# A layered attention kernel with a new order inside each slot: output product and residual in front of the Q projection, and a norm's second parts moved up

## The chip, the cores and the metric

The kernel runs on one core of one Trainium2 chip. The metric is the device time of one execution in microseconds (us). A core has five engines with a queue of instructions each: TensorE (PE in the profile; its weight loads are shown apart as PEld), VectorE (DVE), ScalarE (ACT), GpSimd (POOL) and SyncE (SP), which here issues DMAs. Every engine works its own queue strictly in order, and waits at an instruction until what that needs is there.

## The reference

The input x has 4 sequences (B) of 512 tokens with 128 features. First comes one block of full attention with 16 heads of 64 on a layer norm of x:

```
x = x + softmax(mask(q k^T / 8)) v Wr        with q, k, v = layernorm(x) Wq, Wk, Wv
```

Then x plus the result of six layers. In a layer i, `shift` moves half of the features of each token one token on:

```
q, k, v = split(shift(x) Wqkv[i])                       16 heads of 64
q, k    = rotary(q / |q| * q_scale), rotary(k / |k| * k_scale)
x       = x + local_attention(q, k, v) Wo[i]            windows of 32, each sees itself and the one before
h       = layernorm(shift(x)) * g + b
x       = x + ((h W1a + b1a) * gelu(h W1g + b1g)) W2 + b2
```

All of it is in float32. The change concerns only the six layers.

## The kernel before, in words

Before the layers runs the full attention, up to about 559 us into the span. The layers work in units: a unit is one block of 128 tokens, and there are 6 layers x 4 sequences x 4 blocks = 96 units, numbered n = 0 to 95, in the order layer, sequence, block. T is a unit's block in its sequence (n mod 4), and NT is 4.

The function `slot(n, ...)` is called for n = -1 to 94, and is a software pipeline over units written out by hand: the order of the calls in it is the order of the instructions in each engine's queue (`tc.manual_schedule`), and no planner changes it. In slot n, four units are at work:

- `u` = unit n: its scores (TensorE, L681 and L692; maximum and subtraction on VectorE, L702 and L704; exponents on ScalarE, L710), the transposes of its probabilities P (`transpose_p`, two groups of four), and the product with V (`times_v`, two halves g = 0 and 1 of 64 matmuls, each ended by a reciprocal and a division on VectorE, L733 and L734).
- `prev` = unit n - 1: its output product (`project_out_2`, L749) and the residual (`residual`, L757 on VectorE).
- `nxt` = unit n + 1: the transposes of its Q and K.
- `new` = unit n + 2: its Q, K and V projections (`do_project(new, 0)`, `1`, `2`; L536), the squares of Q and K on ScalarE (`square`, L548), the sums of the squares (L553) and the rotation on VectorE (`rotate`: L558, then L564 into a tile t1), which GpSimd adds up (`add_rotated`, L575), and the division by the norm (`inverse_norms`: L579, L81, L82 on VectorE and a chain of small instructions on GpSimd; `over_norm`, L583 on GpSimd).

Beside this a feed-forward network of a whole sequence (`Ffn`) runs over several slots. After its last unit of attention, in a slot with n mod 4 = 0, `f.shift` (the list `move`) copies the shifted sequence on GpSimd. The three steps of its layer norm (`f.mean`, `f.var`, `f.scale`, the list `norm`) follow in the next three slots, n mod 4 = 1, 2, 3. A step has a first part (a matmul and an instruction or so behind it) and a second part, which is put into the list `later` and issued further on in the same slot: for the mean a square on ScalarE (L104), for the variance a reciprocal square root (two VectorE instructions, L81 and L82, and twelve on GpSimd), for the scale a multiplication by g and addition of b on VectorE (L123), which makes hT. The network's three chunks (L793 and L794, the list `geglu`) come near the ends of the slots n mod 4 = 3, 0, 1, the first of them in the slot of the scale, and its output (L813) in n mod 4 = 2. Slots 0, 1 and 2 have the three steps of another norm, that of the first block's last sequence, which uses no `later` list; slot 93 has the mean of a last network. So the slots with a norm step are n mod 4 = 1, 2, 3 (and 0), and those without are n mod 4 = 0 (and 3).

The PSUM buffers matter here. `two_t(k)` gives one of three two-bank buffers, which change their roles from slot to slot; there is one tile of each. In a slot the scores use `two_t(0)`, Q `two_t(1)`, K `two_t(2)`; V and the first half of times_v use `two_t(0)` again, the second half of times_v and the chunk `two_t(1)`:

```
p = u.p[j] if c0 else two_t(((1, 2, 1), (0, 2, 1), (1, 2, 0))[min(u.n, 2)][j], "ps_proj")
...
o = two_t(g, "ps_att")
```

`one_t()` gives one of two single banks (`ps_one`), for transposes, norm steps and output products. A buffer is used again when all that read it are done.

Of the kernel before, what the change touches and what calls it, by code (L numbers as in the profile page):

```python
# [32 lines left out]
def body(ctx: ExitStack, tc: tile.TileContext, a, out: bass.AP):  # L33
# [37 lines left out]
    def new_xT():  # L71
        return res.tile([P, S], F32, tag="xT", name="xT", bufs=B + 2)
# [416 lines left out]
    def load_part(i, j):  # L489

        w = wts.tile([P, INNER], F32, tag=f"wqkv{j}", name=f"wqkv{j}_{i}")
        nc.sync.dma_start(out=w, in_=a["wqkv"][i, :, j * INNER : (j + 1) * INNER])
        return w
# [19 lines left out]
    def two_t(k, name):  # L513
        k = (part[0] + k) % 3
        return (ps2a if k == 2 else ps).tile([P, 2, 512], F32, tag=f"two{k}", name=name, bufs=1)
# [4 lines left out]
    def heads(ap):  # L520
        return ap.rearrange("p (h d) -> p h d", d=HD)
# [10 lines left out]
    def project(u, j, c0=0, c1=2):  # L532
        p = u.p[j] if c0 else two_t(((1, 2, 1), (0, 2, 1), (1, 2, 0))[min(u.n, 2)][j], "ps_proj")
        u.p[j] = p
        for c in range(c0, c1):
            mm(  # L536
                p[:, c, :],
                lhsT=u.xs[:, u.T * P : (u.T + 1) * P],
                rhs=wpart[j][:, c * 512 : (c + 1) * 512],
                start=True,  # L540
                stop=True,
            )
        if c1 == 2:
            u.p[j] = flat(p)

    def square(u, j):
        u.sq[j] = s2a.tile([P, INNER], F32, tag="t1", name="sq", bufs=4)
        nc.scalar.activation(u.sq[j], u.p[j], AF.Square)  # L548
# [3 lines left out]
            u.ss = small.tile([P, 2 * HEADS], F32, tag="ss", name="ss")  # L552
        nc.vector.tensor_reduce(u.ss[:, j * HEADS : (j + 1) * HEADS], heads(u.sq[j]), AX.X, ALU.add)  # L553

    def rotate(u, j, between=()):
        t0 = u.r[j] = s2a.tile([P, INNER], F32, tag="rot", name="rot", bufs=6)
        lt, pf, half = u.lt, u.p[j], HD // 2
        nc.vector.tensor_tensor(  # L558
            heads(t0), heads(pf), lt[:, u.T, 2 * j].unsqueeze(1).to_broadcast([P, HEADS, HD]), ALU.mult
        )  # L560
        for f in between:
            f()
        t1 = u.t1 = s2a.tile([P, INNER], F32, tag="t1", name="t1", bufs=4)
        nc.vector.tensor_tensor(  # L564
            t1.rearrange("p (h t d) -> p h t d", t=2, d=half),
            pf.rearrange("p (h t d) -> p h t d", t=2, d=half)[:, :, ::-1, :],
            lt[:, u.T, 2 * j + 1]
            .rearrange("p (t d) -> p t d", t=2)
            .unsqueeze(1)
            .to_broadcast([P, HEADS, 2, half]),  # L570
            ALU.mult,
        )

    def add_rotated(u, j):
        nc.gpsimd.tensor_tensor(u.r[j], u.r[j], u.t1, ALU.add)  # L575
# [74 lines left out]
    def transposed(src, g, dst, col0):  # L650

        tp = one_t()
        for c in range(4):
            nc.tensor.transpose(  # L654
                tp[:, c * P : (c + 1) * P], src[:, (4 * g + c) * P : (4 * g + c + 1) * P], ident
            )
        nc.scalar.copy(dst[:, 4 * g : 4 * g + 4, col0 : col0 + P], tp.rearrange("p (c t) -> p c t", c=4))  # L657
# [54 lines left out]
    def transpose_p(u, g):  # L712
        if g == 0:
            u.pT = s2.tile([P, NC, P], F32, tag="pT", name="pT", bufs=2)
        transposed(u.prf, g, u.pT, 0)

    def times_v(u, g):
        if g == 0:
            u.on = s2.tile([P, NC, 2, HD], F32, tag="on", name="on", bufs=1)
        o = two_t(g, "ps_att")  # L720
        for c in range(4):
            for j in range(NW):
                for h in range(2):
                    mm(  # L724
                        o[j * W : (j + 1) * W, h, c * (HD + 1) : (c + 1) * (HD + 1)],
                        lhsT=u.pT[h * HD : (h + 1) * HD, 4 * g + c, j * W : (j + 1) * W],
                        rhs=u.vw[h * HD : (h + 1) * HD, j, 4 * g + c, :],
                        start=True,
                        stop=True,
                    )  # L730
        ov = o[:, :, 0 : 4 * (HD + 1)].rearrange("p a (c d) -> p a c d", d=HD + 1)
        rden = small.tile([P, 2, 4, 1], F32, tag="rden", name="rden")
        nc.vector.reciprocal(rden, ov[:, :, :, HD : HD + 1])  # L733
        nc.vector.tensor_tensor(  # L734
            u.on[:, 4 * g : 4 * g + 4].rearrange("p c a d -> p a c d"),
            ov[:, :, :, 0:HD],
            rden.to_broadcast([P, 2, 4, HD]),
            ALU.mult,
        )
# [11 lines left out]
    def residual(u):  # L751
        if u.T == 0:
            u.xn = new_xT()
        else:
            u.xn = units[u.n - 1].xn
        cols = slice(u.T * P, (u.T + 1) * P)
        nc.vector.tensor_tensor(u.xn[:, cols], u.y[:, 0:P], xT[u.b][:, cols], ALU.add)  # L757
        if u.T + 1 == NT:
            xT[u.b] = u.xn
# [86 lines left out]
    def unit(n):  # L846
        return units[n] if 0 <= n < len(units) else None
# [4 lines left out]
    def begin(u):  # L852

        if u is None or u.T:
            return
        if u.n == 0:
            xs, lt = start
        else:
            xs = shifted(u.b)
            lt = layer_tables(u.i) if u.b == 0 else units[u.n - 1].lt  # L860
        for v in units[u.n : u.n + NT]:
            v.xs, v.lt, v.p = xs, lt, [None] * 3

    def do_project(u, j, c0=0, c1=2):
        project(u, j, c0, c1)
        if c1 == 2 and u.b + 1 == B and u.T + 1 == NT and u.i + 1 < L:
            wpart[j] = load_part(u.i + 1, j)
# [30 lines left out]
    def slot(n, norm, move, geglu):  # L898

        u, prev, nxt, new = unit(n), unit(n - 1), unit(n + 1), unit(n + 2)
        part[0] = -n % 3
        begin(unit(n + 4))
        if u:
            scores(u)
            exponents(u)
        while behind:
            behind.pop(0)()  # L910
        if new:
            do_project(new, 0)
            square(new, 0)
        if n == -1:
            y = one_t()
            project_out1(B - 1, y)
        for f in norm:
            f()
        if prev:
            project_out_2(prev)  # L920
            if prev.b + 1 == B and prev.T + 1 == NT and prev.i + 1 < L:
                wo_w[0] = load_wo(prev.i + 1)


        first = u is not None and u.T == 0
        if prev and not first:
            residual(prev)
        if new and first:
            do_project(new, 1, 0, 1)
            rotate(new, 0)  # L930
            add_rotated(new, 0)
        if prev and first:
            residual(prev)
        for f in move:
            f()
        if u:
            transpose_p(u, 0)
        if new:
            do_project(new, 1, 1 if first else 0, 2 if first else 1)
        if u:  # L940
            transpose_p(u, 1)
        if new and not first:
            rotate(new, 0)
            add_rotated(new, 0)
            do_project(new, 1, 1)
        if new:
            square(new, 1)
        if n == -1:
            residual1(B - 1, y)
        if u:  # L950
            times_v(u, 0)
            times_v(u, 1)
        if new:
            sum_squares(new, 0)
            rotate(new, 1, later)
            later.clear()
            add_rotated(new, 1)
            sum_squares(new, 1)
        if nxt:
            transpose_q(nxt)  # L960
        if new:
            do_project(new, 2, 0, 2 if geglu else 1)
        if new and geglu:
            v_windows(new, follower(new))
        if nxt:
            transpose_k(nxt)
        if new and not geglu:
            do_project(new, 2, 1)
            v_windows(new, follower(new))
        if n == -1:  # L970
            third_step()
        if nxt:
            carry_k(nxt, follower(nxt))
        if new:
            norms = [lambda: inverse_norms(new), lambda: over_norm(new, 0), lambda: over_norm(new, 1)]
            if geglu:
                for f in norms:
                    f()
            else:
                behind.extend(norms)  # L980
        for f in geglu:
            f()
        if u:
            transpose_o(u)

    with tc.manual_schedule():
        begin(units[0])
        later, behind = [], []
# [3 lines left out]
        norm, move, geglu = {k: [f] for k, f in enumerate(late)}, {}, {}  # L992
# [8 lines left out]
        for n in range(NT, end - NT, NT):  # L1001
            f = Ffn(units[n - 1], eng=nc.gpsimd, later=later)
# [27 lines left out]
        u, prev = units[end - 1], units[end - 2]  # L1030
# [144 lines left out]
```

## Time and profile before

| | us |
|---|---|
| median of 3 runs | 2208.52 (2208.43 to 2215.15) |
| the profiled execution | 2208.39 |
| its span, from the first instruction to the last | 2206.6 |
| TensorE busy in the span | 2143.0 (97%) |
| VectorE, ScalarE, GpSimd busy | 1697.0, 1360.4, 1507.8 |

The profile is that of one execution; what the span leaves out of its time is 1.8 us. A slot is counted here from its first scores matmul to that of the next slot. Four slots one after the other take 66.9 us:

| slot (n mod 4) | start | us | PE busy | DVE | ACT | POOL |
|---|---|---|---|---|---|---|
| 32 (0) | 1097.14 | 15.96 | 15.88 | 13.59 | 10.83 | 14.20 |
| 33 (1) | 1113.10 | 16.62 | 16.62 | 14.38 | 12.03 | 11.72 |
| 34 (2) | 1129.72 | 17.61 | 17.61 | 14.63 | 10.54 | 12.55 |
| 35 (3) | 1147.33 | 16.71 | 16.42 | 13.17 | 9.82 | 12.87 |

How to read the rows that follow: in a timeline a row has the start, the duration, the engine, the line of the kernel, the operation, the tiles written and read (out<-in), and the number of instructions that were put together in it; square brackets hold the engine's idle time before it and what ended that. In the groups of lines, behind the bar, stand the busy time, the mean time of one in ns, and the idle time before them with its releasers. A row of waits has the total in us, the number, and the longest. The ends of matmuls are modelled, so that a row's start is the better measure: from the start of one row of TensorE to that of the next is what the first one costs. A float32 matmul counts as two instructions, a transpose as one.

### The profile page before, as it was taken

The page shows a single profiled execution, that of the slowest core. Times are in us where ns is not written, and L with a number is a line of the kernel's source. Part 1 is how long each engine was busy: PE and PEld are TensorE (multiplying, and loading weights), DVE is VectorE, ACT ScalarE, POOL GpSimd, SP SyncE. Part 2 cuts the span into 40 slices and gives each one's busy share as a digit, 9 for nine tenths or more (in the row PEclk, how much of TensorE's full clock was granted, in tenths as well). Part 3 has the DMA queues.
Part 4 walks back from the last instruction along what each step waited for, and adds up shares of the span by engine and source line. Part 5 has one row for each costly group of instructions (what it writes and reads, how often), then busy time and mean ns, then how long its engine had stood idle before and what let it go on. Part 6 is the DMA issues. An engine that isn't in the chain of part 4 may idle for free.

```text
span 2206.6 us, 82386 instructions
## 1 busy us (share of the span) xinstructions
PE 2143.0 (97%) x35150; PEld 1433.3 (65%) x35150; DVE 1697.0 (77%) x2501; ACT 1360.4 (62%) x2589; POOL 1507.8 (68%) x2281
## 2 busy tenths in 40 slices
PE   7999999999999999999999999999999999999997
PEld 5665555564666666666676666666666666666665
DVE  4776767676778887888788878887888788888884
ACT  4665656665556666666666666666666666666663
POOL 2554545455778777777777777777777777777772
PEclk9999999999999999999999999999999999999999
DMA  3000000000332233232332323223332223322220
GB/s 120 1 1 1 1 1 1 1 1 3 75 74 65 64 93 74 62 72 65 95 73 62 77 66 101 62 66 74 74 91 66 65 71 87 81 67 68 62 70 26
DMA packets 91063, 125.76 MB, mean 57 GB/s; under 512 B 25422, under 2 KB 39500, under 8 KB 90700
## 3 DMA queue, kind: packets, MB, share of 16 engines
q1 hardware_dynamic: 89996, 118.79, 21.9%
q8 instruction: 280, 4.59, 0.9%
q10 hardware_dynamic: 704, 1.70, 0.2%
q14 instruction: 83, 0.68, 0.1%
HBM read 20.31 MB, written 1.05 MB: 10 GB/s over the span
## 4 chain that ended last, share of the span: by engine, by line
PE 86%; DVE 9%; POOL 2%; issue 2%; ACT 1%; DMA 0%; SPq 0%; POOLq 0%; ACTq 0%; DVEq 0%
PE ps_proj L536 20%; PE ps_one L654 13%; PE ps_one L749 7%; PE ps_att L692 6%; PE ps_sc L296 6%; PE ps_att L724 5%; PE ps_o L381 5%; PE ps_pt L361 5%; PE ps_proj L793 3%; PE ps_proj L813 3%; PE ps_proj L794 3%; DVE rot L558 2%; DVE ss L553 2%; DVE on L734 1%; PE ps_att L681 1%
## 5 line engine op out<-in xcount | busy, mean ns | idle before, releaser
L536 PE MATMUL ps_proj<-wqkv,xs 128*128 128x512 f32 x1152 | 569.5, 602 | 1.9 <-issue 1.8
L575 POOL TENSOR_TENSOR rot<-rot,t 128x1024 f32<-128x1024 f32 x192 | 453.8, 2364 | 166.3 <-DVE t L564 146.1
L350 POOL TENSOR_TENSOR pr<-pr,den 128x1024 f32<-128x1024 f32 x128 | 240.9, 1893 | 246.4 <-DVE den L347 236.6
L583 POOL TENSOR_TENSOR rot<-rot,ss 128x1024 f32<-128x1024 f32 x192 | 361.8, 1905 | 7.4
L558 DVE TENSOR_TENSOR rot<-ps_proj,lt 128x1024 f32<-128x1024 f32 x192 | 233.7, 1217 | 54.5 <-ACT sq L548 54.2
L536 PEld LDWEIGHTS ps_proj<-wqkv,xs 128*128 128x128 f32 x1152 | 188.3, 190 | 104.3 <-issue 94.8
L710 ACT ACTIVATE pr<-pr 128x1024 f32<-128x1024 f32 x96 | 101.5, 1057 | 228.0 <-DVE pr L704 228.0
L564 DVE TENSOR_TENSOR t<-ps_proj,lt 128x1024 f32<-128x1024 f32 x192 | 233.3, 1215 | 0.0
L553 DVE TENSOR_REDUCE ss<-sq 128x16 f32<-128x1024 f32 x192 | 232.1, 1209 | 0.0
L336 ACT ACTIVATE pr<-ps_sc,nm 128x128 f32<-128x128 f32 (+3 forms) x448 | 220.3, 509 | 11.8 <-DVE nm L323 8.6
L654 PEld LDWEIGHTS ps_one<-ident,rot 128*128 128x128 f32 x1536 | 171.8, 141 | 74.1 <-issue 50.6
L654 PE MATMUL ps_one<-ident,rot 128*128 128x128 f32 x1536 | 205.6, 276 | 11.4 <-POOL rot L583 4.7
L548 ACT ACTIVATE sq<-ps_proj 128x1024 f32<-128x1024 f32 x192 | 195.0, 1016 | 34.1 <-PE ps_proj L536 30.7
L323 DVE TENSOR_REDUCE nm<-ps_sc 128x2 f32<-128x1024 f32 x128 | 156.0, 1219 | 62.8 <-PE ps_sc L311 62.8
L749 PEld LDWEIGHTS ps_one<-aT,wo 128*128 128x128 f32 x1536 | 183.9, 193 | 23.7 <-issue 23.0
L749 PE MATMUL ps_one<-aT,wo 128*128 128x128 f32 x1536 | 190.3, 277 | 0.4 <-DVE rs L111 0.3
L84 POOL TENSOR_TENSOR yt<-y 128x32 f32<-128x32 f32 (+2 forms) x384 | 88.2, 230 | 146.3 <-DVE y L82 100.1
L657 ACT COPY pT<-ps_one 128x512 f32<-128x512 f32 x192 | 112.4, 585 | 97.5 <-PE ps_one L654 97.1
L657 ACT COPY qT<-ps_one 128x512 f32<-128x512 f32 x192 | 103.3, 589 | 108.7 <-PE ps_one L654 108.7
L636 ACT COPY vt<-ps_proj 128x512 f32<-128x512 f32 x192 | 103.1, 589 | 99.5 <-PE ps_proj L536 93.1
L702 DVE TENSOR_REDUCE mx<-ps_att 128x16 f32<-128x1024 f32 x96 | 117.3, 1222 | 60.3 <-PE ps_att L692 59.0
L361 PEld LDWEIGHTS ps_pt<-ident,pr 128*128 128x128 f32 x1024 | 117.4, 141 | 58.6 <-issue 47.7
(173 smaller groups left out, 4092.4 us busy)
## 6 DMA issues: line engine op xcount, KB each, us to landing
vw<-vt SPq DMA_DIRECT2D x1152, 65.0 KB
vw_first<-vt SPq DMA_DIRECT2D x336, 65.0 KB
wqkv<-in_wqkv_dram SPq DMA_DIRECT2D x18, 512.0 KB
wo<-in_wo_dram SPq DMA_DIRECT2D x6, 512.0 KB
w<-in_w_dram SPq DMA_DIRECT2D x6, 341.0 KB
xr<-in_x_dram SPq DMA_DIRECT2D x3, 256.0 KB
scales<-in_scales_dram SPq DMA_DIRECT2D x6, 128.0 KB
w<-in_w_dram SPq DMA_DIRECT2D x12, 64.0 KB
```

What stands on the lines that cost most here:

```text
L336: nc.scalar.activation(self.pr[:, h, cols], self.sc[:, h, cols], AF.Exp, bias=self.nm[:, part_, h : h + 1], accum_out=self.den[:, part_, h ...
L350: nc.gpsimd.tensor_tensor(self.pr, self.pr, self.den[:, 0].unsqueeze(2).to_broadcast([P, 2, S]), ALU.mult)
L361: nc.tensor.transpose(pt[:, k * P : (k + 1) * P], self.pr[:, h, k * P : (k + 1) * P], ident)
L536: mm(p[:, c, :], lhsT=u.xs[:, u.T * P : (u.T + 1) * P], rhs=wpart[j][:, c * 512 : (c + 1) * 512], start=True, stop=True,)
L553: nc.vector.tensor_reduce(u.ss[:, j * HEADS : (j + 1) * HEADS], heads(u.sq[j]), AX.X, ALU.add)
L558: nc.vector.tensor_tensor(heads(t0), heads(pf), lt[:, u.T, 2 * j].unsqueeze(1).to_broadcast([P, HEADS, HD]), ALU.mult)
L564: nc.vector.tensor_tensor(t1.rearrange("p (h t d) -> p h t d", t=2, d=half), pf.rearrange("p (h t d) -> p h t d", t=2, d=half)[:, :, ::-1, :],
L575: nc.gpsimd.tensor_tensor(u.r[j], u.r[j], u.t1, ALU.add)
L583: nc.gpsimd.tensor_tensor(heads(u.r[j]), heads(u.r[j]), u.ss[:, j * HEADS : (j + 1) * HEADS].unsqueeze(2).to_broadcast([P, HEADS, HD]), AL ...
L654: nc.tensor.transpose(tp[:, c * P : (c + 1) * P], src[:, (4 * g + c) * P : (4 * g + c + 1) * P], ident)
L657: nc.scalar.copy(dst[:, 4 * g : 4 * g + 4, col0 : col0 + P], tp.rearrange("p (c t) -> p c t", c=4))
L749: mm(y[:, 0:P], lhsT=wo_w[0][:, c, :], rhs=u.aT[:, c, :], start=(c == 0), stop=(c == NC - 1))
```

## The change

The order of the calls in `slot` is changed, and where `later` is issued.

- In a slot with a norm step, the Q projection with its square is issued behind the norm step, the output product and the residual; before, it was in front of them.
- In a slot without one, Q stays in front. The residual is issued directly behind the output product; before, in slots n mod 4 = 0, it came behind the rotation of Q. The rotation of Q and its `add_rotated` come behind both groups of P's transposes, and `move` in front of them; before, in these slots, rotation and addition came between the two halves of K's projection and `move` after them. P's two groups of transposes stand together between the two halves of K; before, the first group was in front of K's second half and the second behind it.
- The second parts of a norm step (`later`) are issued directly behind the divisions of times_v and in front of the sum of Q's squares; before, between the two instructions of the rotation of K.

The diff:

```diff
-    def rotate(u, j, between=()):
+    def rotate(u, j):
...
-        for f in between:
-            f()
...
-        if new:
+        if n == -1:
             do_project(new, 0)
             square(new, 0)
-        if n == -1:
             y = one_t()
             project_out1(B - 1, y)
         for f in norm:
             f()
+        if new and n >= 0 and not norm:
+            do_project(new, 0)
+            square(new, 0)
+
         if prev:
             project_out_2(prev)
             if prev.b + 1 == B and prev.T + 1 == NT and prev.i + 1 < L:
                 wo_w[0] = load_wo(prev.i + 1)
-
-
-        first = u is not None and u.T == 0
-        if prev and not first:
             residual(prev)
-        if new and first:
-            do_project(new, 1, 0, 1)
-            rotate(new, 0)
-            add_rotated(new, 0)
-        if prev and first:
-            residual(prev)
+        if new and n >= 0 and norm:
+            do_project(new, 0)
+            square(new, 0)
         for f in move:
             f()
-        if u:
+        if u and norm:
             transpose_p(u, 0)
         if new:
-            do_project(new, 1, 1 if first else 0, 2 if first else 1)
+            do_project(new, 1, 0, 1)
         if u:
+            if not norm:
+                transpose_p(u, 0)
             transpose_p(u, 1)
-        if new and not first:
+        if new:
             rotate(new, 0)
             add_rotated(new, 0)
             do_project(new, 1, 1)
-        if new:
             square(new, 1)
...
+        while later:
+            later.pop(0)()
         if new:
             sum_squares(new, 0)
-            rotate(new, 1, later)
-            later.clear()
+            rotate(new, 1)
             add_rotated(new, 1)
```

## The prediction

> **What bounds the kernel now.** I read the page first, then the groups of lines, then who waits for the rows of the normalised activations, and last the timeline of one layer's four slots. A slot is the stretch from one unit's scores to the next unit's; I call its kind n mod 4, so slot 33 is kind 1. From the page:
>
> ```profile
> span 2206.6 us, 82386 instructions
> PE 2143.0 (97%) x35150; PEld 1433.3 (65%) x35150; DVE 1697.0 (77%) x2501; ACT 1360.4 (62%) x2589; POOL 1507.8 (68%) x2281
> PE 86%; DVE 9%; POOL 2%; issue 2%; ACT 1%; DMA 0%; SPq 0%; POOLq 0%; ACTq 0%; DVEq 0%
> L558 DVE TENSOR_TENSOR rot<-ps_proj,lt 128x1024 f32<-128x1024 f32 x192 | 233.7, 1217 | 54.5 <-ACT sq L548 54.2
> ```
>
> TensorE sets the end: its own rows fill the chain. A gain can only be a pause of TensorE that goes, a loss only a pause that is made. The last row is the one I build on: the rotation (DVE) does not start when its projection is ready but when ScalarE's square of the same projection is done; 54.2 us of VectorE's idle time end that way. The waits of TensorE, and those on the normalised activations:
>
> ```profile
> PE ps_att L724 <- issue: 11.0, 10, 1.9
> ...
> who waited for it (us, times):
>   PEld ps_proj L793: 10.5, 20
>   PE ps_proj L793: 5.4, 18
> ```
>
> The first row is pauses that no engine causes, all inside the dense 128 matmuls of times_v; the others are the wait for L123 in the kind-3 slots, the one stall that the change can remove. Slot 33, PE, then ACT, then DVE:
>
> ```profile
> 1114.88 1.98 PE L536 MATMUL ps_proj<-wqkv,xs 128*128 128x512 f32 x4
> 1116.70 1.02 PE L100 MATMUL ps_one<-tmp_t,avg 128*128 128x512 f32 x2
> 1117.56 1.95 PE L749 MATMUL ps_one<-aT,wo 128*128 128x128 f32 x16
> 1119.34 0.60 PE L654 MATMUL ps_one<-ident,pr 128*128 128x128 f32 x4
> 1122.03 1.55 PE L724 MATMUL ps_att<-vw,pT 64*32 64x65 f32 x128
> ...
> 1122.20 1.02 ACT L548 ACTIVATE sq<-ps_proj 128x1024 f32<-128x1024 f32 x1 [0.34 <-PE ps_proj L536]
> ...
> 1119.75 1.21 DVE L558 TENSOR_TENSOR rot<-ps_proj,lt 128x1024 f32<-128x1024 f32 x1
> 1120.88 1.21 DVE L564 TENSOR_TENSOR t<-ps_proj,lt 128x1024 f32<-128x1024 f32 x1
> ```
>
> Q occupies TensorE from 1114.88 to 1116.70 (1.82), the mean 0.86, the output product 1.78. The rotation starts at 1119.75, long after its square. Slot 35 (kind 3) and slot 36 (kind 0):
>
> ```profile
> 1160.65 0.54 DVE L123 TENSOR_SCALAR hT<-hT,vecs 128x512 f32<-128x512 f32 x1
> ...
> 1161.25 1.13 PE L793 MATMUL ps_proj<-hT,w 128*128 128x512 f32 x2 [0.29 <-DVE hT L123]
> ...
> 1169.64 1.01 ACT L548 ACTIVATE sq<-ps_proj 128x1024 f32<-128x1024 f32 x1
> ...
> 1170.68 1.23 DVE L558 TENSOR_TENSOR rot<-ps_proj,lt 128x1024 f32<-128x1024 f32 x1 [2.04 <-ACT sq L548]
> ...
> 1171.62 0.42 PEld L654 LDWEIGHTS ps_one<-ident,pr 128*128 128x128 f32 x4 [0.64 <-ACT pT L657]
> ...
> 1171.82 1.21 DVE L564 TENSOR_TENSOR t<-ps_proj,lt 128x1024 f32<-128x1024 f32 x1
> ...
> 1173.15 0.72 PEld L724 LDWEIGHTS ps_att<-vw_first,pT 64*32 64x32 f32 x64 [0.20 <-ACT pT L657]
> ```
>
> In kind 0 the rotation follows the square, and the second half of times_v (64 of 128) starts at 1173.15, 0.12 after L564 ends (1173.03). That is no accident: times_v(u, 1) takes two_t(1), the buffer in which Q stands (project takes two_t(1) for j = 0), and there is one of it. The label names ScalarE's pT copy, done long before; the late one is L564.
>
> **The skill.** "PSUM — Partial Sum Buffer", PSUM bank collisions: two engines must not touch one bank at once, two reads included, and the compiler's scheduler orders them. The trace agrees: in slot 35 the square ends at 1153.80 and the rotation starts at 1153.84. "SBUF — State Buffer", Who interferes with whom: tensor_scalar in a two-port mode and a GpSimd instruction exclude each other for the whole of the one that came first. It agrees: L579 takes 0.17 us at the least and 1.39 in the middle, ending with POOL's L575. "Runtime: NRT & Kernel Launch", Instruction fetch mechanics: the stream comes in 16 KiB blocks, fetched one ahead; the profile has 280 packets on the instruction queue, and the pauses of the first waits row fit blocks used up faster than fetched.
>
> **Part 1: norm slots (kinds 1 to 3), Q behind norm step, output product and residual.** Nothing is added or removed on TensorE: 1.82 + 0.86 + 1.78 end at 1119.34 in either order. But Q now ends at 1119.34 instead of 1116.70, and the buffer is wanted back at the same time as before. The chain from Q's end: 0.17 to the square (1122.03 to 1122.20 in K's case), 1.02 for it, 0.04 to the rotation (slot 35), 2.34 from L558's start to L564's end (1119.75 to 1122.09), 0.15 to TensorE's second half (0.12 to the weights, 0.03 to the matmul). Sum 3.72. TensorE's own work from 1119.34 to that half: 2.69 to times_v at 1122.03 and 0.67 for its first half: 3.36. So it stalls 0.36. Before, L564 ended at 1122.09 and the half began at 1122.70: hidden with 0.46 to spare; the chain moves by 0.82. Queued behind: everything later on TensorE. Kinds 2 and 3 have the same steps from Q's end on, so the same stall. With a Q to project they are slots 0, 1, 2, 5, 6, 7 ... 89, 90, 91 and 93: 70 slots, 70 x 0.36 = +25.2. Bounds 0.30 and 0.40 from the handover times. What else moves is covered: the norm step needs a ps_one bank that aT's copies free in the first 1.7 us of a slot; the residual is done early on VectorE; square(Q) now stands before pT's first copy on ScalarE, which ends some 0.5 later but still over 0.9 before times_v.
> SP: load_part for Q's weights goes behind this Q and its next user also moves back; load_wo stays in a kind-0 slot. The V window DMAs follow V's copies as before. No DMA price.
>
> **Part 2: second parts directly behind the divisions.** Kind 3: L123 no longer stands behind L553 and L558 (1.21 + 1.22), so hT is ready before the FFN chunk. It removes the gap: kT's transposes to L793 take 1.33 in slot 35 (1159.92 to 1161.25) against 0.87 in slot 33, and the first chunk matmul's 0.96 becomes 0.86. 0.56 x 22 such slots = -12.3. Kind 2: the reciprocal root's POOL chain (12 instructions of 0.2) starts some 2.2 us earlier; it lies beside other work, and must, since the norm's transposes now come 1.8 us earlier in the next slot. Kind 1: the square keeps its place on ScalarE. The catch is the port: t now ends in slot 35 near 1156.7 instead of 1156.19, POOL's L575 (2.36) runs to about 1159.1, and L123, due at 1158.7, waits for it. Its own 0.54 becomes 0.5 to 0.9.
>
> **Part 3: kind 0 slots, residual before, P's two groups together.** The second P group no longer waits (0.64 above) and residual's 0.29 leaves the place behind the rotations; but the end of this slot hangs on exponents, square, rotation, second half of times_v, an order that the edit leaves alone. So it gains nothing. Moving the shift's three POOL instructions (1.4) ahead of L575 only delays add_rotated, and POOL's second L575 follows as before. It loses what kind 3 hands on: there VectorE's tail ends 0.3 later (second division waits for the stalled half) plus 0 to 0.4 for the port, while TensorE is 0.36 - 0.56 = -0.20: VectorE is 0.4 to 0.9 further behind, less about 0.1 to 0.2 of slack at L702. Bounds 0 and 0.7; I take 0.3, nearer the lower as the port's hold may end with POOL. 22 x 0.3 = +6.6.
>
> **Part 4: fetch pauses.** A stall inside times_v gives the fetch time: some 13 of the pauses sit there, each up to 0.36 shorter: -4 (bounds -7 and +4, as the stream's alignment to the blocks may also change).
>
> Sum: 25.2 - 12.3 + 6.6 - 4 = +15.5. The profiled execution took 2208.39 (span 2206.6 and 1.8 around it), 0.13 under the median of 2208.52. Forecast 2224.0.
>
> **Rivals.** A (faster): the rotation need not wait for the square. Then the chain is 0.2 + 2.34 + 0.15 = 2.7, below 3.36, no norm slot stalls, 12.3 is gained in kind 3 and about 0.3 x 22 in kind 0: 2208.5 - 19 = 2189. The norm slots stop stalling if the rotation starts within 0.87 of Q's end (3.36 - 2.34 - 0.15), and the sign turns at 1.0, a stall of 0.14; I put it at 1.23. For: in slot 33 the rotation waited for the residual, so not every row shows the square as its release. Against: slots 35 and 36, where nothing else holds it and it starts at the square's end. Chance 0.09.
> B (no change): a shorter handover, a stall of 0.24, and nothing handed to kind 0: 16.8 - 12.3 - 4, about 2209. Chance 0.13.
> C (worse): in kinds 1 to 3 the second P group gets the bank of the first, as in slot 36 today (0.64 row); pT's copy, now behind the square, ends near 1121.1 and that group, due at 1120.64, costs 0.52 in place of 0.36: 70 x 0.16 = +11, 2235. Against: with the residual in front the other bank is free, and slots 33 and 35 show no such wait. Chance 0.08.
>
> **Numbers.** The forecast's case has 0.70, its own range 2214 to 2235 from the bounds of parts 1, 3 and 4. For 8 in 10 I reach a little into B: 2211 to 2236. About 0.3% (6.6 us) is what a measurement of this kernel tells from no change: faster 0.09, same 0.13, slower 0.70 + 0.08 = 0.78.
>
> **What would show it.** Kinds 1 to 3: L558 directly behind its square in most rows, so L558's idle "<-ACT sq" far above 54 us; a gap of about 0.36 between halves of times_v ended by L564; slots of kinds 1 and 2 near 17.0 and 17.9 (16.62 and 17.5 now). Kind 3: no wait on L123, slot 0.2 shorter; L123 longer than 0.54 beside L575. Kind 0: 0.3 longer. I am wrong if Q's buffer is returned before 3.36 us have passed, or if kind 0's delay exceeds 0.7.

## The result, and the profile after

The changed kernel takes 2248.78 us (median of 6 runs, 2244.49 to 2255.40), the kernel before on the same chip 2210.28 (6 runs, 2207.02 to 2218.76). The ratio is 1.0176, 95% interval 1.0158 to 1.0194: slower by 38.5 us. The forecast was 2224.0 with a range up to 2236, so the direction was right and the size was not. The profiled execution took 2244.49, its span is 2242.7, 36.1 longer than before. From the page of the kernel after, the rows that answer to those of before:

```profile
span 2242.7 us, 82426 instructions
...
PE 2155.0 (96%) x35150; PEld 1434.1 (64%) x35150; DVE 1740.9 (78%) x2501; ACT 1360.3 (61%) x2589; POOL 1510.2 (67%) x2281
...
PE 69%; DVE 22%; ACT 5%; issue 3%; POOL 1%; DMA 0%; SPq 0%; ACTq 0%; DVEq 0%; POOLq 0%
...
L558 DVE TENSOR_TENSOR rot<-ps_proj,lt 128x1024 f32<-128x1024 f32 x192 | 233.9, 1218 | 174.6 <-ACT sq L548 174.6
```

The chain that sets the end went from 86% TensorE to 69%; VectorE has 22% of it (9 before) and ScalarE 5% (1). VectorE's idle time behind a square rose from 54.2 to 174.6. The first row of TensorE's waits is a new one, while the rows on hT (L123) are gone. The second row, the pauses that no engine causes inside times_v, is what it was (11.0 before):

```profile
PE ps_att L722 <- DVE rden L731: 24.7, 77, 0.6
PE ps_att L722 <- issue: 11.1, 9, 1.6
```

Lines from 564 on stand two lower in the changed kernel: t is now L562, add_rotated L573, the maximum in front of the root L577, P's transposes L652, the scores' maximum L700, times_v L722. Slot 33 of the kernel after (kind 1), PE, then ACT, then DVE:

```profile
1134.11 0.60 PE L652 MATMUL ps_one<-ident,pr 128*128 128x128 f32 x4
...
1136.80 0.86 PE L722 MATMUL ps_att<-vw,pT 64*32 64x65 f32 x64
1137.93 0.85 PE L722 MATMUL ps_att<-vw,pT 64*32 64x65 f32 x64 [0.27 <-DVE rden L731]
...
1134.37 1.02 ACT L548 ACTIVATE sq<-ps_proj 128x1024 f32<-128x1024 f32 x1 [0.86 <-PE ps_proj L536]
...
1135.43 1.22 DVE L558 TENSOR_TENSOR rot<-ps_proj,lt 128x1024 f32<-128x1024 f32 x1 [2.21 <-ACT sq L548]
1136.57 1.21 DVE L562 TENSOR_TENSOR t<-ps_proj,lt 128x1024 f32<-128x1024 f32 x1
```

This is the chain of the prediction, link by link. Q is done at 1134.11; 0.26 later its square starts, 1.02 long; 0.04; the two rotations from 1135.43 to 1137.78; 0.15 later the second half of times_v. The halves are 1.13 apart where the first half's own work is 0.67 (the spacing of the halves in slots of kinds 1 and 2 before): a stall of 0.46. TensorE's bracket names the reciprocal of the first half (L731), which runs in the same moment; that it is the rotation instead is shown by the run with the free square below.

How the span's 36.1 come together. I take a slot as the 30th percentile of its kind over slots 8 to 94, which leaves single pauses aside:

| | before | after | difference, us |
|---|---|---|---|
| kind 0, 22 slots | 16.04 | 16.71 | +14.7 |
| kind 1, 22 slots | 16.62 | 17.06 | +9.7 |
| kind 2, 22 slots | 17.48 | 17.96 | +10.6 |
| kind 3, 21 slots | 16.69 | 16.54 | -3.2 |
| pauses above these values | 20.2 | 19.0 | -1.2 |
| slots 0 to 7 | 130.56 | 135.34 | +4.8 |
| in front and behind | | | +0.8 |

The sum is 36.2. Of the 4.8 of slots 0 to 7, slots 6 and 7 have 4.7; the last section shows why. The largest single surprise is kind 0. From slots 35 and 36 of the kernel after:

```profile
1174.45 0.90 DVE L123 TENSOR_SCALAR hT<-hT,vecs 128x512 f32<-128x512 f32 x1
...
1179.90 1.39 DVE L577 TENSOR_SCALAR ss<-ss 128x32 f32<-128x32 f32 x1
...
1182.42 1.21 DVE L700 TENSOR_REDUCE mx<-ps_att 128x16 f32<-128x1024 f32 x1
...
1189.43 0.85 PE L722 MATMUL ps_att<-vw_first,pT 64*32 64x65 f32 x64 [0.52 <-DVE rden L731]
```

Slot 36 starts at 1179.70. VectorE is still busy with the root of the unit before, and the maximum of the new scores starts 2.72 into the slot (2.09 in the median slot of kind 0 before); exponents, square, rotation and the second half of times_v follow it.

### The profile page after: what moved, and what is told of

Its sections match the earlier page's. It is cut to its first block, busy times and chain, and to the rows that moved or that the text cites. A ratio compares the mean times of both kernels' runs of the same rounds, so it can differ in the third digit from the quotient of the medians.

```text
span 2242.7 us, 82426 instructions
## 1 busy us (share of the span) xinstructions
PE 2155.0 (96%) x35150; PEld 1434.1 (64%) x35150; DVE 1740.9 (78%) x2501; ACT 1360.3 (61%) x2589; POOL 1510.2 (67%) x2281
## 4 chain that ended last, share of the span: by engine, by line
PE 69%; DVE 22%; ACT 5%; issue 3%; POOL 1%; DMA 0%; SPq 0%; ACTq 0%; DVEq 0%; POOLq 0%
PE ps_proj L536 12%; PE ps_one L652 10%; PE ps_one L747 6%; DVE rot L558 6%; PE ps_sc L296 5%; DVE t L562 5%; PE ps_o L381 5%; PE ps_att L690 5%; PE ps_pt L361 5%; PE ps_att L722 4%; ACT sq L548 4%; PE ps_proj L811 3%; DVE ss L553 2%; PE ps_proj L791 2%; PE ps_proj L792 2%
## 5 line engine op out<-in xcount | busy, mean ns | idle before, releaser
L573 POOL TENSOR_TENSOR rot<-rot,t 128x1024 f32<-128x1024 f32 x192 | 453.4, 2364 | 235.2 <-DVE t L562 182.1
L558 DVE TENSOR_TENSOR rot<-ps_proj,lt 128x1024 f32<-128x1024 f32 x192 | 233.9, 1218 | 174.6 <-ACT sq L548 174.6
L708 ACT ACTIVATE pr<-pr 128x1024 f32<-128x1024 f32 x96 | 101.5, 1057 | 236.9 <-DVE pr L702 236.9
L562 DVE TENSOR_TENSOR t<-ps_proj,lt 128x1024 f32<-128x1024 f32 x192 | 232.9, 1213 | 0.0
L652 PEld LDWEIGHTS ps_one<-ident,rot 128*128 128x128 f32 x1536 | 172.0, 141 | 70.2 <-issue 45.4
L652 PE MATMUL ps_one<-ident,rot 128*128 128x128 f32 x1536 | 205.9, 277 | 6.9 <-POOL rot L581 3.1
L747 PEld LDWEIGHTS ps_one<-aT,wo 128*128 128x128 f32 x1536 | 184.8, 193 | 24.7 <-issue 24.0
L722 PEld LDWEIGHTS ps_att<-vw,pT 64*32 64x32 f32 x9216 | 103.5, 105 | 91.5 <-ACT pT L655 52.5
L652 PEld LDWEIGHTS ps_one<-ident,pr 128*128 128x128 f32 x768 | 92.5, 141 | 97.9 <-issue 56.2
```

The costliest lines, as they stand in the source:

```text
L558: nc.vector.tensor_tensor(heads(t0), heads(pf), lt[:, u.T, 2 * j].unsqueeze(1).to_broadcast([P, HEADS, HD]), ALU.mult)
L562: nc.vector.tensor_tensor(t1.rearrange("p (h t d) -> p h t d", t=2, d=half), pf.rearrange("p (h t d) -> p h t d", t=2, d=half)[:, :, ::-1, :],
L652: nc.tensor.transpose(tp[:, c * P : (c + 1) * P], src[:, (4 * g + c) * P : (4 * g + c + 1) * P], ident)
L747: mm(y[:, 0:P], lhsT=wo_w[0][:, c, :], rhs=u.aT[:, c, :], start=(c == 0), stop=(c == NC - 1))
```

## The experiments

Times are medians, and each ratio is against the kernel before on the same chip, with its 95% interval. The theories: R, Q's buffer comes back late (the prediction's chain); V, VectorE's queue sets the end from kind 3 into kind 0; P, the SBUF port that VectorE and GpSimd share.

**The three parts apart.** Four kernels: the change with part 1 undone, and the kernel before with each part alone.

```
e1:  -  if new and n >= 0 and not norm: do_project(new, 0); square(new, 0)   (behind the norm step)
     -  if new and n >= 0 and norm: do_project(new, 0); square(new, 0)       (behind the residual)
     +  if new: do_project(new, 0); square(new, 0)                           (in front, every slot)
```

> The kernel after with part 1 alone undone: the Q projection and its square in front in every slot. Theory R (the returned buffer): the loss in the norm slots is the chain Q, square, rotation, second half of times_v. Then kinds 1 and 2 fall back from 17.06 and 17.96 to about 16.6 and 17.5 and kind 3 from 16.54 to about 16.1. Kind 0 decides between two sub-theories. H (handed on): kind 0 loses because VectorE comes late out of kind 3; then it falls from 16.8 to about 16.2 and the whole comes to about 2200. O (its own edits): the order inside kind 0 costs the 0.65 itself; it stays at 16.8 and the whole comes to about 2214. Rival P (the port): the loss comes from the second parts behind the divisions, which stand beside POOL's addition; then undoing part 1 gives back little, and the time stays above 2230.

2217.98 (2216.09 to 2223.32), ratio 1.0037 (1.0023 to 1.0050). Kinds 1, 2 and 3 fell to 16.59, 17.47 and 16.13, as R has it. Kind 0 fell only to 16.56, between the two sub-theories, so this run alone doesn't settle it.

```
e2:  -  if new: do_project(new, 0); square(new, 0)
     +  if new and not (n >= 0 and norm): do_project(new, 0); square(new, 0)
     and, behind the residual,
     +  if new and n >= 0 and norm: do_project(new, 0); square(new, 0)
```

> The kernel before with part 1 alone: in slots with a norm step Q and its square stand behind norm step, output product and residual. Theory R: all three norm kinds gain a stall of 0.45 in front of the second half of times_v, 70 x 0.45 = +31, about 2241; the gap in front of the network's first chunk in kind 3 stays (0.5). Theory H adds up to 0.5 in each of 22 kind-0 slots: 2241 to 2252. Rival P: within 6 of the time before (2210).

2241.20 (2235.87 to 2242.74), ratio 1.0127 (1.0111 to 1.0143). Kinds 1 and 2 stand at 17.05 and 17.96, with 1.13 between the halves of times_v in the median slot; kind 3 rose by only 0.22, as part of its wait for hT now lies under the stall. Kind 0 is at 16.05: part 1 hands nothing on. Theory H falls in the form that I gave it.

```
e3:  +  while later: later.pop(0)()            (behind the divisions)
     -  rotate(new, 1, later)
     +  rotate(new, 1)
```

> The kernel before with part 2 alone: the second parts of a norm step directly behind the divisions. Prediction's part 2: the gap of 0.56 in kind 3 goes, 22 slots, -12, about 2198, with hT taking 0.5 to 0.9 in place of 0.54 beside POOL's addition. Rival P: the tiny VectorE instruction of the reciprocal root waits for POOL's addition in kind 2, the rotation of K ends later and the scores of the next slot wait: 2205 to 2220.

2210.60 (2206.19 to 2214.83), ratio 0.9987 (0.9975 to 0.9999): hardly anything, though kind 3 fell by 0.57, to 16.12, just the 0.56 of part 2. Kind 0 rose by 0.45, to 16.49, and took it back. VectorE's queue in slot 36, first in the kernel before, then with part 2 alone:

```profile
1163.49 1.39 DVE L579 TENSOR_SCALAR ss<-ss 128x32 f32<-128x32 f32 x1
...
1166.16 1.23 DVE L702 TENSOR_REDUCE mx<-ps_att 128x16 f32<-128x1024 f32 x1
```

```profile
1163.55 1.39 DVE L579 TENSOR_SCALAR ss<-ss 128x32 f32<-128x32 f32 x1
...
1166.06 1.21 DVE L702 TENSOR_REDUCE mx<-ps_att 128x16 f32<-128x1024 f32 x1
```

The same times to 0.1 us, but the slot begins at 1164.04 in the first and at 1163.44 in the second. TensorE came 0.60 sooner and VectorE didn't: L123 was moved within VectorE's queue, not taken out of it.

```
e4:  residual directly behind the output product, move in front, both groups
     of P's transposes between K's halves, rotation of Q behind them (kind 0)
```

> The kernel before with part 3 alone: in kind 0 the residual directly behind the output product, the shift ahead of the rotation, both groups of P's transposes together between the halves of K, and the rotation behind them. Prediction and theory H: no change, 2207 to 2213, kind 0 stays near 16.1. Theory O: kind 0 is longer by about 0.6 on its own, 22 x 0.6 = +13, about 2223.

2219.51 (2212.90 to 2221.83), ratio 1.0034 (1.0023 to 1.0046). Kind 0 itself stays at 16.04, as predicted, and yet some 7 us are lost. They lie in slots 13, 29, 45, 61 and 77, which are 9.0 above their kind's value in sum (2.1 before). Each follows a slot of kind 0 in which GpSimd also makes the next layer's rotation table. Slot 61 of this run begins at 1587.56; POOL, then DVE, then PE:

```profile
1587.10 4.70 POOL L575 TENSOR_TENSOR rot<-rot,t 128x1024 f32<-128x1024 f32 x2
...
1587.10 0.18 DVE L579 TENSOR_SCALAR ss<-ss 128x32 f32<-128x32 f32 x1
1587.31 2.23 DVE L81 TENSOR_SCALAR yt<-ss 128x32 int32<-128x32 int32 x1
1589.57 2.27 DVE L82 TENSOR_SCALAR y<-yt 128x32 int32<-128x32 int32 x1
...
1592.42 1.21 DVE L702 TENSOR_REDUCE mx<-ps_att 128x16 f32<-128x1024 f32 x1
...
1596.03 0.66 PE L654 MATMUL ps_one<-ident,pr 128*128 128x128 f32 x4 [2.08 <-ACT pr L710]
```

Two of GpSimd's additions stand back to back, and two VectorE instructions of 0.2 us each last as long as one of them: one slips in between the additions only to meet the next. The scores' maximum starts 4.9 into the slot, and TensorE waits 2.08 for the exponents. The trace of before has no instruction of these two lines in the layers over 1.6 us; this one has 6, and so has the kernel after. In the kernel after less of it reaches TensorE: its waits for the exponents (L708 there) come to 4.2 us, in e4 (L710) to 7.4, before to 0.9.

The medians of parts 1, 2 and 3 alone are 28.9, -1.7 and 7.2 from 2212.3: 34 of the 38.5.

**The shift at its old place.** Which of part 3's moves brings the additions together?

```
e10 (against e4):  -  for f in move: f()          in front of P's transposes
                   +  for f in move: f()          behind add_rotated(new, 0)
```

> The kernel before with part 3, but the shift (move) behind the rotation of Q and its addition, as before; residual, P's groups and the rotation stand as in the change. Part 3 alone came to 2219.5 with its slots of kind 0 unchanged; in the slots 13, 29, 45, 61, 77 (one a layer, behind the slot in which GpSimd also makes the next layer's table) the exponents came late. Theory S (the shift): with it in front, GpSimd's two additions of kind 0 stand back to back, and VectorE's two small instructions of the reciprocal root each lose the port to one of them (2.23 and 2.27 in slot 61); with the shift between them again that is gone: 2208 to 2213. Rival G (P's groups and the late rotation): the time stays at 2217 to 2221 and TensorE waits for exponents in those slots as in part 3 alone (7.4 in all).

2210.13 (2202.24 to 2216.68), ratio 1.0000 (0.9989 to 1.0011). Theory S: the loss is gone, and no instruction of L81 or L82 is over 1.6 us. The shift's 1.4 us between the additions is what let VectorE through. In slot 61 of this run, POOL and then DVE:

```profile
1583.42 2.38 POOL L575 TENSOR_TENSOR rot<-rot,t 128x1024 f32<-128x1024 f32 x1
...
1587.33 2.35 POOL L575 TENSOR_TENSOR rot<-rot,t 128x1024 f32<-128x1024 f32 x1
...
1586.08 0.56 DVE L82 TENSOR_SCALAR y<-yt 128x32 int32<-128x32 int32 x1
```

**The square taken out of the chain.**

```
e5:  -  nc.scalar.activation(u.sq[j], u.p[j], AF.Square)
     +  nc.scalar.activation(u.sq[j], u.p[j] if j else <the table u.lt>, AF.Square)
```

> The kernel after, but Q's square reads the rotation's table in SBUF (as many elements) in place of the projection, so the sums of squares of Q are of other data; the square costs ScalarE the same and does not hold Q's buffer. Theory R: without 1.02 for the square the chain from Q's end is 0.2 + 2.34 + 0.15 = 2.7, below TensorE's own 3.36, so the stall in the norm kinds is gone: kinds 1 and 2 fall from 17.06 and 17.96 to 16.6 and 17.5, kind 3 from 16.54 to about 16.1; kind 0, whose end hangs on the same chain behind the exponents, falls too, by up to 0.7: 2249 - 31 - 5 to 15, about 2205. Rival P (the stall comes from VectorE's late start for another reason, such as the port or the residual): the norm kinds stay within 0.1 of 17.06 and 17.96, the whole stays above 2235.

This kernel leaves out the squares of Q itself: ScalarE squares as many elements of the rotation's table. 2202.77 (2195.78 to 2213.48), ratio 0.9969 (0.9956 to 0.9982): 46 us below the kernel after, with the same order and as much work on every engine. Kinds 0 to 3 stand at 15.85, 16.59, 17.48 and 16.07. From the groups of lines, and the timeline of slot 33 of this run:

```profile
L558 DVE TENSOR_TENSOR rot<-ps_proj,lt 128x1024 f32<-128x1024 f32 x192 | 233.9, 1218 | 67.6 <-PE ps_proj L536 66.5 <-ACT sq L548 1.0
```

```profile
1124.52 1.51 PE L722 MATMUL ps_att<-vw,pT 64*32 64x65 f32 x128
...
1125.42 0.21 DVE L731 RECIPROCAL rden<-ps_att 128x8 f32<-128x8 f32 x1 [1.05 <-PE ps_att L722]
```

The rotation now waits for the projection, and times_v is one row of 128 without a break. Its second half starts at about 1125.2 (1124.52 and 0.67), before the first half's reciprocal at 1125.42. So that half never needed the reciprocal, and the bracket of the kernel after named the wrong instruction. R is shown, the link from square to rotation included: the condition of my rival A, made true by hand (and more, as the square does not read Q at all), gives 2203. In kind 0 the maximum still starts late, 2.55 into the median slot, and the slot is short all the same. So the late maximum costs time only through the chain of exponents, square and rotation behind it.

**VectorE's queue or the port.** The second part of the scale (L123, hT) goes to ScalarE, in the kernel after and in the kernel before; or it stays on VectorE, but clear of GpSimd's addition.

```
e6, e7:  -  nc.vector.tensor_scalar(h, h, g, b, ALU.mult, ALU.add)
         +  nc.scalar.activation(h, h, AF.Identity, bias=b, scale=g)
e8:      later between sum_squares(new, 0) and rotate(new, 1), in the kernel before
```

> The kernel after with the scaling that makes hT (line 123) on ScalarE in place of VectorE, at the same place in the order. Theory V: VectorE's queue from kind 3's divisions over the rotation of K and POOL's addition to the maximum of kind 0 sets the end there, and what TensorE gains in kind 3 it waits for in kind 0. Without 0.54 to 0.91 in that queue, kind 0 falls from 16.72 to 16.05 or so, kinds 1, 2 and 3 stay: 2249 - 22 x 0.65 = about 2235. Rival (kind 0 is late by its own order together with the late Q of the slots before): kind 0 stays above 16.5, about 2247.

> The kernel before with the scaling that makes hT on ScalarE in place of VectorE. Theory V: kind 3 loses its gap of 0.57, 16.70 to 16.13, and kind 0 keeps 16.05, since VectorE's queue is shorter by 0.54 as well: 22 x 0.57 = -12.5, about 2198, ahead of both kernels. Rival: ScalarE's row comes in the way of the copies behind the transposes of Q; then kind 3 stays above 16.4 and the time above 2204.

> The kernel before with the second parts of a norm step between the sum of Q's squares and the rotation of K: about 1.2 behind the divisions, when POOL's addition is done or nearly so, and still 1.2 ahead of before. It tells theory V from the port. Theory V: VectorE has the same work up to the end of K's rotation, so that end stays, kind 3 gains about 0.57 and kind 0 gives 0.45 back, as in the kernel with part 2 alone: 2205 to 2211. Port: with hT at its 0.54 clear of POOL's addition nothing is handed on; kind 0 stays at 16.05 and the time is about 2198.

e6: 2237.87 (2230.93 to 2243.35), ratio 1.0129 (1.0098 to 1.0160). Kind 0 falls to 16.06, the others stay: with L123 off VectorE's queue, nearly all of the 0.67 is gone. e7: 2199.63 (2193.63 to 2213.36), ratio 0.9958 (0.9946 to 0.9970): kind 3 at 16.12, kind 0 at 16.09, the gap of kind 3 saved and kept. e8: 2210.51 (2205.59 to 2219.84), ratio 1.0006 (0.9996 to 1.0016): L123 has its 0.54 in the median and nobody waits for it, and still kind 0 stands at 16.48. So L123's own meeting with GpSimd's addition is not what hands the time on: it is enough that L123 stands in the queue in front of the rotation's second part t, as it did before, while TensorE now comes sooner. (Kind 3 comes down only to 16.30 here. In slot 34 the small instructions of the norm's root now run on GpSimd directly in front of its addition, L579 behind them takes 2.31, and the maximum of slot 35 starts 2.30 into it.)

But the port is not out of the chain. Slot 36 of e8 begins at 1168.85; POOL, then DVE:

```profile
1167.79 2.36 POOL L575 TENSOR_TENSOR rot<-rot,t 128x1024 f32<-128x1024 f32 x1 [3.57 <-DVE t L564]
...
1168.81 1.39 DVE L579 TENSOR_SCALAR ss<-ss 128x32 f32<-128x32 f32 x1
...
1171.32 1.22 DVE L702 TENSOR_REDUCE mx<-ps_att 128x16 f32<-128x1024 f32 x1
```

The addition starts when t is done. L579 ends with it, at 1170.20, and the rest of the root, one instruction of the network and the maximum follow. L579 takes 0.17 at the least, so the addition holds it for some 1.2, an estimate; that is more than the 0.5 by which the maximum is late. So the chain is VectorE's queue up to t, then the addition, then the root that it holds. Whether anything would be handed on without this hold no run shows, since e9 below takes L123 and the start of the root off VectorE together.

In the full change L123 takes 0.90 in the median (0.59 in e3), since with the stall it meets GpSimd's addition for longer, and kind 0 is at 16.71 against 16.49 with part 2 alone. That the second comes from the first is argued from the sizes, not shown.

**A version ahead of both.** If VectorE's queue and the port are what costs, the start of each root can leave VectorE as well.

```
e9 (against e7):
-  nc.vector.tensor_scalar(ti, v.bitcast(I32), 1, None, ALU.logical_shift_right)
-  nc.vector.tensor_scalar(y.bitcast(I32), ti, -1.0, 1597463007.0, ALU.mult, ALU.add)
+  eng.tensor_scalar(y.bitcast(I32), v.bitcast(I32), -0.5, 1597463007.0, ALU.mult, ALU.add)
-  nc.vector.tensor_scalar(u.ss, u.ss, 1e-24, None, ALU.max)
+  nc.gpsimd.tensor_scalar(u.ss, u.ss, 1e-24, None, ALU.max)
```

> The kernel before with hT on ScalarE, as in the run before, and the start of each reciprocal root on GpSimd: the maximum there, and the shift and the subtraction as one multiplication and addition on the integers. VectorE has three instructions less in a slot, 1.6 in the mean of the kernel before with their waits for the port, and GpSimd two more of about 0.25. If VectorE's queue and the port still cost something with hT on ScalarE (kind 0's end hangs on the maximum, the late exponents of single slots): kind 0 falls from 16.1 by up to 0.3, waits for exponents go, 2185 to 2195. If GpSimd's queue becomes the bound (its division by the norm ends later and Q's transposes wait for it): 2200 to 2215. If neither: 2200 as without it.

2193.04 (2188.52 to 2197.27), ratio 0.9915 (0.9898 to 0.9932), the fastest of all. VectorE's busy time is 1543.6 in place of 1697.0, the chain of its profile is TensorE to 90%. But the expected fall of kind 0 did not come (16.01): of the gain of 6.6 over e7, 5.8 lies in slots 0 to 7 of the profiled executions (123.9 against 129.7).

**The change with both repairs.** e11 is the kernel after with the edits of e6 and e9.

> The kernel after with both repairs: hT on ScalarE and the start of the reciprocal roots on GpSimd. If the accounts are right, what the change loses outside its part 1 is all in VectorE's queue and its port: kind 0 falls to about 16.05, the long waits for the port go, and only the stall of the norm slots stays. 2193 of the repaired kernel before plus 70 x 0.46 = +32: about 2225, kinds 1 and 2 still at 17.05 and 17.95, kind 3 at 16.55. If the parts hinder each other beyond that: above 2232. If the stall also needs VectorE's queue full: below 2215.

2225.72 (2221.19 to 2230.31), ratio 1.0076 (1.0053 to 1.0098), kinds 0 to 3 at 16.06, 17.05, 17.93 and 16.53. Against e9 that is +32.7, where 70 stalls of 0.46 make 32.2: the accounts close, within the 5 us that this run's interval leaves.

**The square in front of the exponents.** A test of the prediction's chain through kind 0.

```
e12 (against e9):  +  if u and new and not norm and not behind: do_project(new, 0); square(new, 0)
                      exponents(u)
```

> The repaired kernel before (hT on ScalarE, roots begun on GpSimd), and in the slots without a norm step (kind 0) Q's square is issued in front of the exponents in place of behind them. It asks whether the end of kind 0 hangs on exponents, square, rotation, second half of times_v, as the prediction has it. If so, the rotation no longer waits for the exponents, the 0.3 by which that half is late goes (halves of times_v 0.96 apart where 0.67 is their own work), and kind 0 falls from 16.05 to about 15.75: 22 x 0.3 = -6.6, about 2187. If the exponents, later by some 0.35, then hold the transposes of P instead: kind 0 stays within 0.1 of 16.05, about 2193.

2213.00 (2205.07 to 2223.63), ratio 1.0012 (0.9998 to 1.0027), 20 us above e9: worse than either expectation. Kind 0 rose to 16.91. The chain was cut as meant: t ends at 7.26 in the median slot in place of 8.94, and the second half of times_v starts 2.67 after it. But see ScalarE and TensorE in slot 36 of this run:

```profile
1165.40 1.02 ACT L546 ACTIVATE sq<-ps_proj 128x1024 f32<-128x1024 f32 x1 [2.17 <-PE ps_proj L534]
1166.44 1.28 ACT L708 ACT_TABLE_LOAD   x1
...
1168.84 0.66 PE L652 MATMUL ps_one<-ident,pr 128*128 128x128 f32 x4 [0.90 <-ACT pr L708]
```

The load of the exponents' table, which lay in ScalarE's idle time in front of them, now stands behind the square. The exponents come 1.60 later in the median slot, where I had counted 0.35, and the load is the difference. "ScalarE: Activation LUTs", What ACT_TABLE_LOAD costs, gives about 1283 ns for it, and the trace agrees (1.28). The expectation left it out.

## Why the prediction was right in direction and wrong in size

- **Part 1, the stall of the norm slots (+25.2).** The mechanism is right: square, rotation, Q's buffer (e2, e5). The size is 0.46 in place of 0.36, 70 x 0.46 = +32.2. (Added up over these slots, the halves of times_v lie 30.6 further apart than their own work in the kernel after, and 1.3 before.) The mis-sized term is the first link: I took 0.17 from Q's end to the square, from K's square in slot 33, and it is 0.26 for Q behind the residual (1134.11 to 1134.37); 0.26 + 1.02 + 0.04 + 2.35 + 0.15 is 3.82 against 3.36 of TensorE's own work. My bounds of 0.30 and 0.40 were the spread of one handover seen at another place. Why it is longer here no run shows.
- **Part 2 (-12.3).** Right in its slot: 0.57 per kind-3 slot in e3. The wait on hT is gone, and L123 takes 0.90, the upper end of 0.5 to 0.9. In the full change kind 3 is 0.15 shorter, 0.20 predicted. What I put at nothing is the norm's root in kind 2, moved up likewise: in slot 6 it meets GpSimd's addition, slot 6 becomes 2.2 longer, and slot 7, which starts with the clock at half, 2.4 (last section).
- **Part 3, what kind 3 hands on (+6.6).** This step failed most: I took 0.3 per slot, and it is 0.67, +14.7. My own sum, 0.4 to 0.9 further behind less 0.1 to 0.2 of slack, gives 0.2 to 0.8, which holds the 0.67; I went to 0.3 because GpSimd's hold of the port might end early. It does not. VectorE's work up to t stays the same when L123 moves within it, so the addition behind t and the root that it holds end when they did before (e3, e8), and what TensorE gains in kind 3 it waits for in kind 0. Of 0.57 gained, 0.12 is kept in e3, as much as the slack that I subtracted at the maximum.
- **Part 3, the shift's move, costed at nothing ("only delays add_rotated").** Wrong: about 7 us in e4, none in e10; in the full change some 3 us, by TensorE's waits for the exponents (4.2 against 0.9). Moving it took the gap out from between two of GpSimd's additions, and the tiny instructions behind them in VectorE's queue lost the port twice.
- **Part 4, shorter fetch pauses (-4).** Not seen. The pauses that no engine causes inside times_v are 11.0 in 10 before and 11.1 in 9 after, so in these two traces the stalls did not shorten them. No run shows what these pauses are.
- **The rivals.** A's condition (a rotation that needn't wait) does turn the sign, as e5 shows. B's shorter handover is the opposite of what came. C (a wait of the second P group) was not seen: both groups take 0.44.

The terms as measured: 32.2 for part 1, -12.5 for part 2 (22 x 0.57), 14.7 for kind 0 and about 0 for the pauses sum to 34.4; the rest to 36.1 is single pauses, those of slots 6 and 7 among them. The two mis-sized terms, 7.0 and 8.1, and the 4 that did not come are 19.1 of the 20.6 by which 36.1 passes the forecast's 15.5. The range was too narrow as well: the sums of all lower and of all upper bounds would be about 2210 and 2244, and the result lies above even that.

## What to carry to other kernels

When two engines meet once in every turn of a loop, a pause taken from one of them is kept only if the other's chain up to the next meeting gets shorter too. Here taking the instruction off VectorE's queue did it (hT to ScalarE: -0.4%), and moving it forward in that queue kept almost nothing (-0.1%). A buffer's release is a chain with every reader in it, so count from the producer's end to the last reader's end before moving the producer back. And before work is moved on one engine, look at what its old place kept apart on another.

## What the runs showed of the hardware that I had not expected

- A VectorE instruction of 0.2 us can cost 2.3, and two in a row 4.5, when GpSimd has long instructions back to back. "SBUF — State Buffer", Who interferes with whom, states the lock; that a second tiny instruction meets the next lock at once is what slot 61 above adds.
- A wait of TensorE can cost twice. Slot 7 of the kernel after begins 2.90 late, through a port wait of 2.28 in the slot before, in the norm's root that part 2 moved up; the rows, and the granted clock (the column in front of the last two) from the table of windows:

```profile
668.29 2.28 DVE L82 TENSOR_SCALAR y<-yt 128x4 int32<-128x4 int32 x1
...
674.01 0.63 PE L679 MATMUL ps_att<-band,ident 64*32 64x512 bf16 x8 [2.90 <-DVE t L562]
```

```profile
668.00:673.70 5.70, 3.11 (x20) 2.15 (x19) 5.67 (x5) 3.43 (x7) 4.72 (x13) 1.00 0.15 35
673.80:677.10 3.30, 3.09 (x140) 2.74 (x140) 1.89 (x3) 0.00 (x0) 2.49 (x2) 0.50 0.37 84
```

Over the 3.3 us of the second row the clock is at half. "TensorE: Matmul & The Clock Gate", Part 1, gives half rate behind an idle window of about 3.4 us; here a wait of 2.90 was enough.
- The name in a wait's bracket can be a bystander: the 24.7 us put down to the reciprocal L731 belong to the rotation that ended just before it (e5).
